# A planner in place of a hand-written order: recorded calls, byte-level dependences, steps placed by urgency

## Chip, cores and metric

One core of a Trainium2 chip runs the kernel. The metric is the device time of one launch in microseconds (us); the time of a kernel is the median of its runs. A core has five engines that work side by side, each through its own queue in order: TensorE (PE) for matrix products, VectorE (DVE), ScalarE (ACT), GpSimd (POOL), and SyncE (SP), which here issues nearly all transfers (DMA). An engine waits on semaphores for what others produce, and everything behind a waiting instruction on the same engine waits with it. Matrix products are written to PSUM, eight banks of 128 partitions by 512 floats; everything else on chip lies in SBUF.

## What is computed

A gated feed-forward layer with quantization, for 4 batches of 1024 tokens, D = 512, FF = 2048:

```python
scale = cond @ norm_w.T + 1.0
ms = jnp.mean(x * x, axis=-1, keepdims=True)
h = x * (scale[:, None, :] * jax.lax.rsqrt(ms + EPS))
u = h @ up_w.T                                  # 512 -> 2 * 2048
val, gate = jnp.split(u, 2, axis=-1)
h = val * jax.nn.gelu(gate, approximate=False)
hq = act_quant(h)                               # per token: 127 / max|h|, rounded
wq = weight_quant(down_w)                       # -1, 0, 1 times mean|down_w|
y = hq @ wq.T                                   # 2048 -> 512
return y + x
```

## The kernel before

Values for the first product are split in two f16 parts (high and low), so that one product takes several f16 matmuls. The weights `up_w` are scaled by powers of two, transposed and split while the first batch runs, and kept in DRAM (`s_dram`) for the later batches, from where they are loaded block by block into `SXY`.

The first batch multiplies directly (`plain`, L577; `plain_first`, L620). Its 16 column blocks j are walked by `first_batch(j)`, which also prepares the weights of blocks to come, the quantized `down_w` (L439, L440), and the tokens of the second batch (`Tokens`: `norm`, `scale`, `high`, `low`, `turn`). The later three batches use a Strassen scheme with seven products of 6 matmuls for each block (`slot(g)`, products at L562); PSUM banks have the tags A (2 buffers), B (1), E (2) and po (3). Each slot takes about 9 us of PE and has three places x, y and z at which other work is woven in: the largest magnitude per token (`pair_max`, L691 to L698), quantizing the batch before (`quant_scale` L754, `quant_round` L758, `quant_up` L762, `quant_down` L766), the token steps of the next batch, and in slots 10 to 13 the down products of the batch before (`Pair`, L833).

The order is written out by hand. The functions are called in the order in which every engine is to carry out its steps, and `Filler` queues distribute DVE's and ACT's lesser steps over slots by budgets in microseconds (`SLOT_US = 9.07`, for example). SP's transfers stand in the same order.

Some steps that the text below speaks of:

- At the start (L879 to L992): x is loaded, its squares are summed (`first_sum`, L899), a small Newton step gives the row factors (`rsqrt_start`, the last line is L911), `first_scale` (L916 and L918) scales four blocks of tokens, one of them on POOL, `first_turn` (L923) transposes them on PE into the banks `ptx`, `w_scale` (L295 on ACT, L297 on POOL) scales the first weights. `keep_warm` (L939) lets PE multiply zeros meanwhile.
- `plain_half`: the products of a half block, then `ACT` with Gelu (L601), then DVE's product of value and gate (L605), which reads PSUM. In the slots the same is done at L640 to L679 (L660 reads the bank A of the block before).
- `token_max` (L712): the largest magnitude over partitions, an all-reduce on POOL, two for a batch (halves h = 0 and 1). `token_scale` (L717, L723) turns it into quantizing factors on DVE.
- `get_ready` (L705): an all-reduce of a 1-element tile `ready`, whose result nothing reads. It is called in slot 0 of the second batch and in the last slot of each of the later batches.
- `Tokens.norm` sums squares on ACT (L496) and takes the root on POOL (L466, L467); `Tokens.scale` goes on with ACT (L504) and POOL (L506) or DVE (L509). `Tokens.low` is L545.

Tiles come from pools with rings of buffers for each tag; semaphores are set by the framework from the accesses of each tile.

Of the kernel before, what the change touches and what calls it, by code (L numbers as in the profile page):

```python
# [1 line left out]

# [44 lines left out]
}  # L47


@with_exitstack  # L50
def glu_quant_kernel(
    ctx: ExitStack,
# [6 lines left out]
    out: bass.AP,  # L59
):  # L60
    nc = tc.nc
    PE, ACT, DVE, POOL, SP = nc.tensor, nc.scalar, nc.vector, nc.gpsimd, nc.sync
    B, S, D = x.shape
    C = cond.shape[1]
    FF = down_w.shape[1]
# [7 lines left out]
    xv = xf.rearrange("(b h a r) d -> b a r h d", b=B, h=2, a=NA)  # L73

    cpool = ctx.enter_context(tc.tile_pool(name="const", bufs=1))
    sm = ctx.enter_context(tc.tile_pool(name="small", bufs=2))
    wpool = ctx.enter_context(tc.tile_pool(name="work", bufs=2))
    psum = ctx.enter_context(tc.tile_pool(name="psum", bufs=2, space=PSUM))

    ident = cpool.tile([P, P], F32, name="ident")  # L80
    neghalf = cpool.tile([P, 4], F32, name="neghalf")
# [70 lines left out]
    def po_bank(name, shape=None):  # L152
        return bank("po", 3, shape, name)
# [553 lines left out]
    def am_tile(b):  # L707
        return wpool.tile([P, 2 * TOK], F32, name=f"am_{b}", tag="am", bufs=1)
# [59 lines left out]
    def rows_of(b, h, a):  # L768
        r = b * S + h * TOK + a * P
        return slice(r, r + P)  # L770
# [18 lines left out]
    def down_end(b, h, a, po, xr, dq, c=slice(None), eng=SP):  # L789
        n = h * NA + a  # L790
        DVE.scalar_tensor_tensor(xr, po, dq[:, n : n + 1], xr, ALU.mult, ALU.add)
        eng.dma_start(out=of[rows_of(b, h, a), c], in_=xr)
# [86 lines left out]
    DVE.memset(eps, EPS)  # L879
# [79 lines left out]
    am = w_largest(0, 1, 2)  # L959
# [317 lines left out]
    for b in range(1, B):  # L1277
        dve, act = Filler(), Filler()
        gains(b)
        am = am_tile(b - 1)  # L1280
# [14 lines left out]
        steps = {}  # L1295
        pairs = {}
        if b + 1 < B:
# [185 lines left out]
    work = list(half_steps(0))  # L1483
# [27 lines left out]
    work = [f for _, f in token_scale(1, am)] + [lambda: token_turn(b, am, 1, 2)]  # L1511
    work += list(half_steps(1))
    bring_dq = [token_undo(b, dq, 0, 1)]
    for h in range(2):
# [15 lines left out]
        work = []  # L1530
# [12 lines left out]
_INS = ["x", "cond_256", "L0_cond_norm_w", "L0_cond_up_w", "L0_cond_down_w"]  # L1543
_OUTS = [((4, 1024, 512), "float32")]
# [23 lines left out]
```

## Time and profile before

| | |
|---|---|
| time, median of 3 runs | 737.53 us (736.88 to 738.68) |
| span of the profiled execution | 734.4 us |
| its own time | not given apart from the three runs; their median lies 3.1 us above the span |
| PE busy | 723.1 us (98% of the span), granted clock 1.000 |
| DVE, ACT, POOL busy | 597.2, 391.0, 200.3 us |
| bytes moved | 115.73 MB, mean 158 GB/s |

The span runs from the first to the last instruction. Busy is the time in which an engine carried out at least one instruction. A waiting list names for each pair of places how long the first stood until the second released it: total us, how many times, the longest. In rows of the timeline the first number is the start and the second the duration, both in us; x12 means that many instructions merged into one row, and the bracket gives the idle time of the engine just before and what ended it. A q behind an engine's name (POOLq) means its instruction queue. `<-issue` stands for idle time for which the profile shows no releaser.

### The profile page before, as it was taken

The numbers are of one execution on the slowest core, as the hardware profiler recorded it, in microseconds if no ns is written. First come the engines' busy times: TensorE is split into PE (matmuls) and PEld (weight loads), VectorE is DVE, ScalarE is ACT, GpSimd is POOL, SyncE is SP. The second block draws the span as 40 slices with busy tenths as digits, with TensorE's granted clock in tenths as the row PEclk, the third lists the DMA queues.
The fourth block names the chain that finished last, engine by engine and source line by source line (L and its number), as shares of the span: only waits on it lengthen the run. The fifth ranks groups of instructions, "written<-read, shape, count | busy, mean of one in ns | idle before, by whom it ended". The sixth has DMA issues, their size and how long they took to land.

```text
span 734.4 us, 10192 instructions
## 1 busy us (share of the span) xinstructions
PE 723.1 (98%) x3684; PEld 361.6 (49%) x3684; DVE 597.2 (81%) x833; ACT 391.0 (53%) x635; POOL 200.3 (27%) x213
## 2 busy tenths in 40 slices
PE   7999999999999999999999999999999999999997
PEld 3554444444444445665444445666444444445744
DVE  6968989877888899797689887787678888755897
ACT  5768657664235676535335666453433665332274
POOL 1487947886100031450010030461020000000100
PEclk9999999999999999999999999999999999999999
DMA  7759989998433545777833556757933445542253
GB/s 232 251 201 135 285 240 244 255 252 222 137 101 99 130 104 172 172 173 172 207 101 100 130 101 171 179 148 164 232 108 102 92 99 104 103 103 90 92 182 115
DMA packets 179566, 115.73 MB, mean 158 GB/s; under 512 B 141750, under 2 KB 147767, under 8 KB 179516
## 3 DMA queue, kind: packets, MB, share of 16 engines
q1 hardware_dynamic: 179226, 114.76, 60.8%
q8 instruction: 29, 0.48, 0.3%
q10 hardware_dynamic: 290, 0.33, 0.2%
q14 instruction: 21, 0.17, 0.1%
HBM read 58.93 MB, written 23.09 MB: 112 GB/s over the span
## 4 chain that ended last, share of the span: by engine, by line
PE 90%; DVE 5%; DMA 2%; POOL 1%; ACT 1%; issue 1%; SPq 0%; DVEq 0%; POOLq 0%
PE A L562 34%; PE E L562 17%; PE po L833 8%; PE B L562 8%; PE pv L577 7%; PE pg L577 7%; PE po_end L782 4%; PE po L782 1%; DMA H<-in_x_dram 1%; PE pw L305 1%; DMA sc<-rows_dram 1%; DVE H L320 1%; DVE nx L545 1%; DVE wam L269 1%; DVE H L605 1%
## 5 line engine op out<-in xcount | busy, mean ns | idle before, releaser
L562 PEld LDWEIGHTS <-SXY 128*128 128x128 f16 x2016 | 197.3, 98 | 232.2 <-issue 0.6
L562 PE MATMUL A<-R,SXY 128*128 128x512 f16 x1152 | 266.2, 379 | 0.0
L562 PE MATMUL E<-R,SXY 128*128 128x512 f16 x576 | 140.0, 379 | 0.1
L660 DVE SCALAR_TENSOR_TENSOR H<-A,sg,t 128x512 f32<-128x512 f32 x48 | 36.0, 750 | 73.2 <-PE A L562 73.0
L712 POOL PARTITION_ALL_REDUCE am<-R x8 | 14.4, 1795 | 232.0 <-DVE R L698 232.0
L754 DVE TENSOR_TENSOR H<-H,am 128x1024 f32<-128x1024 f32 x64 | 76.2, 1217 | 0.0
L577 PEld LDWEIGHTS <-SXY 128*128 128x128 f16 x462 | 45.2, 98 | 55.5 <-issue 1.7
L673 ACT ACTIVATE t<-t,sg 128x512 f32<-128x512 f32 x48 | 34.6, 721 | 69.0 <-DVE t L670 68.8
L562 PE MATMUL B<-R,SXY 128*128 128x512 f16 x288 | 70.0, 379 | 0.0
L696 DVE TENSOR_REDUCE gm<-H 128x512 f32<-128x1024 f32 x56 | 69.0, 1231 | 1.0
L577 PE MATMUL pg<-R,SXY 128*128 128x512 f16 x252 | 57.8, 379 | 0.0
L833 PE MATMUL po<-wd,R 128*128 128x256 fp8e4 (+1 forms) x448 | 56.8, 275 | 0.0
L833 PEld LDWEIGHTS <-R 128*128 128x128 bf16 (+1 forms) x480 | 47.0, 98 | 12.8
L657 ACT ACTIVATE t<-B,sg 128x512 f32<-128x512 f32 x48 | 33.0, 688 | 35.9 <-PE B L562 35.9
L466 POOL TENSOR_SCALAR ssq<-ssq 128x2 f32<-128x2 f32 x12 | 3.2, 268 | 176.5 <-ACT xt L496 124.1
L577 PE MATMUL pv<-R,SXY 128*128 128x512 f16 x210 | 49.9, 379 | 1.1 <-DVE H L605 1.1
L640 ACT COPY t<-A 128x512 f32<-128x512 f32 x48 | 28.0, 583 | 39.8 <-PE A L562 39.4
L648 ACT COPY B<-A 128x512 f32<-128x512 f32 x48 | 27.4, 572 | 38.4 <-PE A L562 38.0
L762 ACT ACTIVATE H<-H 128x1024 f32<-128x1024 f32 x38 | 39.9, 1050 | 14.2 <-DVE H L754 14.1
L652 ACT COPY v<-E 128x512 f32<-128x512 f32 x48 | 28.1, 586 | 31.6 <-PE E L562 27.8
L577 PEld LDWEIGHTS <-R 128*128 128x128 f16 x282 | 27.6, 98 | 34.7 <-issue 2.6
L698 DVE TENSOR_TENSOR R<-R,gm 128x512 f32<-128x512 f32 x56 | 42.3, 755 | 1.3
(203 smaller groups left out, 1013.4 us busy)
## 6 DMA issues: line engine op xcount, KB each, us to landing
SXY<-s_dram SPq DMA_DIRECT2D x66, 256.0 KB, 3.4
SXY<-s_dram SPq DMA_DIRECT2D x18, 384.0 KB, 3.2
H<-in_L_cond_up_w_dram SPq DMA_DIRECT2D x13, 512.0 KB, 3.8
s_dram<-SXY SPq DMA_DIRECT2D x14, 384.0 KB, 3.1
xr<-in_x_dram SPq DMA_DIRECT2D x19, 256.0 KB, 3.0
out_dram<-xr SPq DMA_DIRECT2D x19, 256.0 KB, 2.4
H<-in_x_dram SPq DMA_DIRECT2D x8, 512.0 KB, 5.6
R<-in_L_cond_down_w_dram SPq DMA_DIRECT2D x8, 512.0 KB, 6.7
```

What stands on the lines that cost most here:

```text
L562: PE.matmul(o, s[:, w, k, :], tv[:, :, c, l, k, :], start=start and n == 0, stop=stop and n == len(TERMS) - 1, skip_group_check=True,)
L577: PE.matmul(ps, a[k // 2][:, w, k % 2, :], XP[:, l, k, h * TOK : (h + 1) * TOK], start=n == 0, stop=n == len(terms) - 1,)
L652: ACT.copy(cur["v"], cur["E"])
L657: ACT.activation(cur["t1"], pb, AF.Gelu, scale=gain(g, 1))
L660: DVE.scalar_tensor_tensor(h_half(g - 1, 0), prev["A"], gain(g - 1, 0), prev["t1"], ALU.mult, ALU.mult)
L673: ACT.activation(prev["t2"], prev["t2"], AF.Gelu, scale=gain(g - 1, 1))
L696: DVE.tensor_reduce(gm[0], v, AX.X, ALU.max, apply_absolute_value=True)
L698: return [largest, lambda: DVE.tensor_tensor(m, m, gm[0], ALU.max)]
L754: DVE.tensor_tensor(v, v, r.to_broadcast([P, 2, TOK]), ALU.mult)
L762: ACT.activation(v, v, AF.Copy, bias=MAGIC)
L782: PE.matmul(po.rearrange("p (y c o) -> p y c o", c=2, o=P), q[:, a, h, j], wd8[:, :, j // n, j % n, :, y0:y1].rearrange("p c o y -> p y c o"),
L833: PE.matmul(po, w[:, j], m, start=start and j == 0, stop=stop and j == n - 1, skip_group_check=True,)
```

## The change

The engines are replaced by recorders. Every call (`PE.matmul(...)`, `SP.dma_start(...)`) is written down as a step with its line, its operands, a price in microseconds, and the earlier steps that it depends on, by which 64-byte pieces of a tile (1024-byte pieces of DRAM) they write and read. At the end of the kernel `order` plans all steps six times over and keeps the plan whose PE ends first, and `emit` issues the steps in the order of planned start. The calls themselves and their recorded order stay as they were. The pools become `Rings`, which hand out the same numbers of buffers as fixed tiles.

In a round, `needed` gives each step its latest time: for PE the start in the round before, for other steps the end of the plan, and for all of them no later than what their users need. `place` takes the steps by that time. PE's steps are put one behind another; a step of another engine goes to the first gap on its engine that holds it, from the end of its last operand on. A transfer takes a gap on SP for its issue, and one on a single line of transfers.

```diff
-    PE, ACT, DVE, POOL, SP = nc.tensor, nc.scalar, nc.vector, nc.gpsimd, nc.sync
+    book = Plan()
+    PE, ACT, DVE, POOL, SP = book.engines(nc)
...
-    sm = ctx.enter_context(tc.tile_pool(name="small", bufs=2))
-    wpool = ctx.enter_context(tc.tile_pool(name="work", bufs=2))
-    psum = ctx.enter_context(tc.tile_pool(name="psum", bufs=2, space=PSUM))
+    banks = ctx.enter_context(tc.tile_pool(name="psum", bufs=1, space=PSUM))
+    sm = Rings(cpool, {})
+    wpool = Rings(cpool, {"xn": 1024, "xt": 1024, "am": 1024, "nx": 1792, "v": 512, "gm": 512})
+    psum = Rings(banks, {"A": 512, "B": 512, "E": 512, "po": 512})
...
-    ctx.enter_context(tc.manual_schedule())
     start_t = sm.tile([P, 1], F32, name="start_t", bufs=1)
...
     down_end(b, h, a, po, xr[:, c], dq, c, ACT)
+    ctx.enter_context(tc.manual_schedule())
+    book.emit(book.order())
...
+class Plan:
...
+    def add(self, eng, method, real, args, kwargs):
...
+        s.cost, s.wait = price(eng, method, writes, reads, args, kwargs)
...
+        f = args[2] if method == "activation" else None
+        if f in (AF.Sqrt, AF.Gelu):
+            if f != self.table[0]:
+                deps.update(self.table[1])
+                self.table = f, []
+            elif self.table[1]:
+                deps.add(self.table[1][0])
+            self.table[1].append(s.n)
...
+    def needed(self, clock):
+        for s in reversed(self.steps):
+            s.late = clock if s.eng != "PE" else s.start
+            for t in s.after:
+                s.late = min(s.late, t.late - lag(s, t) - s.wait - s.cost)
+
+    def place(self):
+        steps = self.steps
+        used = {e: Line() for e in ("PE", "ACT", "DVE", "POOL", "SP", "DMA")}
+        last = 0.0
+        for s in sorted(steps, key=lambda s: (s.late, s.n)):
+            t = max((steps[d].end + lag(steps[d], s) for d in s.deps), default=0.0)
+            if s.eng == "PE":
+                t = max(t, last)
+                last = t + s.cost
+                s.start, s.end = t, last
+                continue
+            s.start = used[s.eng].put(t, s.cost)
+            s.end = s.start + s.cost
+            if s.wait:
+                s.end = used["DMA"].put(s.start + 1.2, s.wait) + s.wait + LANDING
+        return last
...
+ROUNDS, LANDING = 6, 1.5
...
+def price(eng, method, writes, reads, args, kwargs):
...
+    if eng == "PE":
+        f32 = any(v.dtype == F32 for v in reads)
+        return (max(n, 64) * (2 if f32 else 1) / 2.4 + 2.5) / 1e3, 0.0
+    if eng == "ACT":
+        return 0.1 + wide * 0.00092 + (0.07 if method != "copy" else 0) + (0.2 if "accum_out" in kwargs else 0), 0.0
+    if eng == "DVE":
+        if wide <= 32:
+            return 0.2, 0.0
...
+        if method == "tensor_tensor" and not psum:
+            if all(v.dtype in (BF16, F16) for v in reads):
+                return 0.1 + wide * 0.0006, 0.0
+            if out.dtype == F16:
+                return 0.1 + wide * 0.0013, 0.0
+        return 0.1 + wide * 0.00107, 0.0
+    if eng == "POOL":
+        if method == "partition_all_reduce":
+            return 1.8 if wide > 1 else 0.4, 0.0
...
```

Here `n` and `wide` are elements for each partition, of the result and of the widest operand. `lag` is 0.2 us after PE, 0.08 us ahead of POOL, 0.05 us elsewhere, and 0 within an engine.

More of the change, by code (lines that the diff above doesn't have):

```diff
@@ L1 @@
+import bisect
+import sys
+import types
 from contextlib import ExitStack
@@ L47, with _runs @@
 }
+GRAIN = 64
+def _runs(v):
+    name, dims, size = v.name, list(v.ap), mybir.dt.size(v.dtype)
+    if str(v.space).endswith("DRAM"):
+        base = v.offset
+        free = dims
+        grain = 1024
+    else:
+        base = v.offset % dims[0][0] if dims[0][0] else v.offset
+        free = dims[1:]
+        grain = GRAIN
+    free = sorted((abs(s), n) for s, n in free if n > 1 and s)
+    run = size
+    while free and free[0][0] * size <= run:
+        s, n = free.pop(0)
+        run = max(run, s * size * (n - 1) + run)
+    starts = [base * size]
+    for s, n in free:
+        starts = [a + s * size * i for a in starts for i in range(n)]
+    return name, {g for a in starts for g in range(a // grain, (a + run - 1) // grain + 1)}
@@ new lines, in _free, with _at_line, call, __init__ @@
+def _free(v):
+    n = 1
+    for d in v.shape[1:]:
+        n *= d
+    return n
+def _at_line(line):
+    def call(method, args, kwargs):
+        return method(*args, **kwargs)
+    return types.FunctionType(call.__code__.replace(co_firstlineno=line - 1), globals())
+class Step:
+    __slots__ = (
+        "n", "eng", "do", "args", "kwargs", "line", "cost", "wait", "deps", "after", "late", "start", "end",
+    )
+class Engine:
+    def __init__(self, plan, name, real):
+        self._plan, self._name, self._real = plan, name, real
+    def __getattr__(self, method):
+        real = getattr(self._real, method)
+        def record(*args, **kwargs):
+            self._plan.add(self._name, method, real, args, kwargs)
+        return record
@@ new lines, with __init__, put, lag @@
+ROUNDS, LANDING = 6, 1.5
+class Line:
+    def __init__(self):
+        self.spans = []
+    def put(self, t, cost):
+        v = self.spans
+        n = bisect.bisect_right(v, (t, 1e9))
+        if n and v[n - 1][1] > t:
+            t = v[n - 1][1]
+        while n < len(v) and v[n][0] < t + cost:
+            t = v[n][1]
+            n += 1
+        v.insert(n, (t, t + cost))
+        return t
+def lag(s, t):
+    if s.eng == t.eng:
+        return 0.0
+    if s.eng == "PE":
+        return 0.2
+    return 0.08 if t.eng == "POOL" else 0.05
```

112 lines of the change are left out of this document (added).

## The prediction

> **What bounds the kernel now.** I read the page's first lines, then who TensorE (PE) waited for, then the busy time by stretches of 20 us, and last the timeline of the places at which PE stood.
>
> ```profile
> span 734.4 us, 10192 instructions
> PE 723.1 (98%) x3684; PEld 361.6 (49%) x3684; DVE 597.2 (81%) x833; ACT 391.0 (53%) x635; POOL 200.3 (27%) x213
> ...
> PE pv L577 <- DVE H L605: 3.2, 4, 1.8
> PE ptx L923 <- DVE wam L147: 1.8, 1, 1.8
> PE pz L939 <- DVE eps L879: 1.4, 1, 1.4
> PE pg L620 <- ACT SXY L329: 0.7, 1, 0.7
> PE pg L620 <- ACT R L927: 0.2, 1, 0.2
> ...
> core 0: us, PE busy (x) PEld busy (x) DVE busy (x) ACT busy (x) POOL busy (x), PEclk, DMA share, GB/s
> 0.00:20.00 20.00, 15.76 (x74) 7.77 (x75) 14.07 (x62) 12.45 (x26) 3.18 (x8) 1.00 0.77 241
> 100.00:120.00 20.00, 17.24 (x79) 7.62 (x78) 19.73 (x24) 9.90 (x16) 17.14 (x18) 1.00 0.76 199
> 120.00:140.00 20.00, 19.60 (x92) 8.79 (x90) 17.91 (x22) 15.37 (x25) 15.85 (x16) 1.00 1.09 265
> ```
>
> PE is busy for 723.1 of 734.4 us, and an order can't make its 3684 matmuls fewer. What is left is 11.3 us: 4.2 in the first 20 us, 2.8 and 0.4 in the two stretches around 120 us, and the tail after the last matmul:
>
> ```profile
> 730.59 0.48 DVE L791 SCALAR_TENSOR_TENSOR R<-po_end,dq_end,R 128x256 f32<-128x256 f32 x1 [0.89 <-PE po_end L782]
> 731.11 0.35 ACTq L792 DMA_DIRECT2D out_dram<-R  x1
> ```
>
> The tail of about 3.8 us (734.4 less 730.6) is one DVE step and one transfer, which no order shortens. So the most that placing can win is the 3.2 us that PE waits for DVE at L605 (PSUM is not yet read out because DVE is behind) and something of the start. Against this stands everything that the planner doesn't know of. The median of the runs is 737.53; no separate time is given for the profiled execution, so I take 737.5 for it, 3.1 us over its span, and do the sum on the span.
>
> **What the planner does.** PE's steps keep about the order in which they are recorded, and every other step goes to the first free gap on its engine after its operands are ready, the most urgent first. Within an engine the result is still one fixed queue: a step that is late in truth holds all behind it. Its prices are close to the trace for the large steps (a 512-wide matmul 215.8 ns; 12 of them take 2.59 us in the chain of waits, `PE A L562 x12`). I look for steps whose true cost isn't in a price.
>
> ```profile
> 196.80 2.59 PE A L562 x12
> ```
>
> **The start: POOL's code.** `get_ready` (L705) is a 1-element all-reduce that the hand order puts ahead of the real all-reduces of L712. The trace shows what it is for:
>
> ```profile
> L705 POOLq MODIFY_POOL_CONFIG  x6: 6/13/18, 178.6 to 498.6; - x6
> L466 POOLq MODIFY_POOL_CONFIG  x4: 88/88/88, 202.7 to 373.9; - x4
> 177.76 0.67 POOL L369 TENSOR_TENSOR R<-H,R 128x256 f16<-128x256 f32 x1
> 184.54 0.38 POOL L705 PARTITION_ALL_REDUCE ready<-ready  x1 [6.11 <-issue]
> 198.47 1.81 POOL L712 PARTITION_ALL_REDUCE am<-R  x1 [13.55 <-DVE R L698]
> ...
> 334.74 0.38 POOL L705 PARTITION_ALL_REDUCE ready<-ready  x1 [6.45 <-issue]
> ```
>
> After ordinary steps the first all-reduce comes 6.11 to 6.45 us late, waiting for nothing but the configuration change ahead of it; the change back (L466) follows the last all-reduce. The same can be seen at the very start for ordinary steps:
>
> ```profile
> L918 POOLq MODIFY_POOL_CONFIG  x2: 11/11/11, 0.8 to 0.8; - x2
> L918 POOLq EVENT_SEMAPHORE  x1: 2574/2574/2574, 7.7 to 7.7; - x1
> 10.09 0.16 DVE L911 SCALAR_TENSOR_TENSOR rs<-newton,rs 128x4 f32<-128x4 f32 x1
> 10.43 0.91 POOL L918 TENSOR_SCALAR H<-H,rs 128x512 f32<-128x512 f32 x1 [10.00 <-DVE rs L911]
> 10.82 1.97 PE L923 MATMUL ptx<-ident,H 128*128 128x128 f32 x16 [1.80 <-DVE wam L147]
> 11.32 0.70 POOL L297 TENSOR_SCALAR H<-H,iv 128x512 f32<-128x512 f32 x1
> 13.90 0.39 PE L620 MATMUL pg<-R,SXY 128*128 128x512 f16 x1 [0.68 <-ACT SXY L329]
> ```
>
> The configuration for ordinary steps is asked for at 0.8 and POOL's queue goes on at 7.7: 6.9 us, hidden today because rs comes at 10.25.
>
> Now the change. The four `get_ready` calls depend on `ready` alone, and nothing depends on them. The planner therefore gives them the last urgency, and then the first gap on POOL that holds 0.4 us, which is the start, where POOL has nothing until L918. All four move there, past everything that POOL does. POOL's true queue is then: load for the all-reduce from 0.8, 6.1 to 6.9 us; four all-reduces at 0.38, 1.5 us; load for ordinary steps, 6.1 to 6.9 us; and only then L918, at 14.5 to 16.1 instead of 10.43. That is 4.1 to 5.7 late; I take 5.0. L918 scales one of the four blocks whose transposes (L923) fill each `ptx` bank, and L297 scales the first weights, so the first product at 13.90 waits for both, and PE has nothing else to do. Cover: none. **+5.0**, bounds 0 (the change back is instant, which the trace can't tell, since POOL has nothing to do for long after it) and 5.7.
>
> **The wait for DVE around 100 to 132 us.**
>
> ```profile
> 106.49 1.48 DVE L284 TENSOR_SCALAR sg<-sw,dx 128x2 f32<-128x2 f32 x1
> 112.42 2.67 DVE L545 TENSOR_TENSOR nx<-xt,nx 128x1024 f16<-128x1024 f32 x1
> 115.00 0.74 DVE L605 SCALAR_TENSOR_TENSOR H<-pv,sg,g 128x512 f32<-128x512 f32 x1
> 115.80 2.75 PE L577 MATMUL pv<-R 128*128 128x512 f16 x12 [1.78 <-DVE H L605]
> ```
>
> L605 is what PE waits for, and L545 is wanted only in the next batch. By urgency L605 goes first wherever it is ready, which removes the 1.78 us and its like. But a step isn't interrupted once begun, and the planner prices this L545 at 1.43 and the 2-element L284 at 0.2, where the trace has 2.67 and 1.48 (POOL is busy 17.14 of those 20 us). Part of the wait stays: **-2.5**, bounds -3.2 and 0. A later start of PE helps too, since weights arrive meanwhile.
>
> **The later all-reduces.** With `get_ready` gone from its places, L712 itself asks for the load. It is free if POOL has been idle some 6.5 us before L712 is ready, as in 178 to 198 now. But the planner also pulls ordinary steps ahead: the token steps of the next batch run as soon as their buffers are free, where the hand order has them here:
>
> ```profile
> 258.48 0.19 POOL L466 TENSOR_SCALAR ssq<-ssq 128x2 f32<-128x2 f32 x1 [55.77 <-ACT xt L496]
> ...
> 367.63 1.81 POOL L712 PARTITION_ALL_REDUCE am<-R  x1 [32.51 <-DVE R L698]
> 373.84 0.75 DVE L660 SCALAR_TENSOR_TENSOR H<-A,sg,t 128x512 f32<-128x512 f32 x1 [1.77 <-PE A L562]
> 376.23 2.75 PE L562 MATMUL A<-R,SXY 128*128 128x512 f16 x12
> ```
>
> If these fall close to an all-reduce, before 198 or 367, a load of 6.1 to 6.9 us is exposed, and DVE's L717, next in its queue, holds the PSUM read-outs behind it. The read-out L660 ends at 374.59, and its bank is written again by the second half of the 12 matmuls from 376.23, at 377.5: 2.9 us to spare. An exposed load so costs PE 0 to 3.5 us each, not its whole length. Two boundaries at 1 each: **+2**, bounds 0 and 7. The third I take as covered, its token steps being over long before.
>
> **Remaining differences.** ACT's table load for Gelu, SP's one queue of transfers and DVE's short steps at 0.2 cost something where the plan left no room: **+1**, bounds -1 (transfers earlier) and 4. The sum: 734.4 + 5.0 - 2.5 + 2 + 1 = 739.9, and 3.1 around it give 743.0. With all lower bounds it is 733.3, with all upper ones 754.2.
>
> **One rule of the skill against this change.** The start of the trace has PE slow at first and then fast:
>
> ```profile
> 3.55 2.31 PE L939 MATMUL pz<-H 128*128 128x512 f16 x5
> 7.34 1.69 PE L939 MATMUL pz<-H 128*128 128x512 f16 x7
> ```
>
> The five warm-up matmuls at 3.55 take 0.46 us each, the seven at 7.34 take 0.24. Here PE's longest pause after that is 1.8 us; in the changed kernel it would stand from about 12 to 16 or 17. If that sends it back to 0.46, then at most the 5.9 us that it needed here (1.4 to 7.34) run at half speed: up to +2.9, so 745.9 in place of 743.0. The Trainium skill (TensorE: Matmul & The Clock Gate, "What's actually happening") says that an idle window of about 3.4 us halves the clock until as long a busy one has passed; by that figure I estimate +1.7, and no run here shows it yet.
>
> **Rivals.** First, faster: the loads stay covered, because the change back is instant, and L605 no longer waits. 737.5 - 3.2, and about 0.9 from the two short waits at L620, is 733.4. For it: prices that fit the trace; against it: the 6.9 us at the start.
>
> Second, no difference: 737.5. Either gains and losses cancel, or the planner ends near the hand's order because the recorded order and its buffers leave little freedom.
>
> Third, clearly slower by one mechanism: ACT stands behind POOL at the turn of a batch. A token step's scale (L504) waits for rs of POOL:
>
> ```profile
> ACT xn L504 <- POOL rs L467: 6.7, 2, 3.9
> 204.61 0.59 ACT L640 COPY t<-A 128x512 f32<-128x512 f32 x1 [1.84 <-PE A L562]
> 205.71 2.75 PE L562 MATMUL A<-R,SXY 128*128 128x512 f16 x12
> ```
>
> The copy L640 ends at 205.20 and PE goes on with that bank at 205.71, so ACT has about 0.5 us to spare. If the plan puts token norms right after an all-reduce, rs comes a load later than planned, 6.1 to 6.9 us, L504 stands at ACT's head and the copies behind it stop PE for some 6 us. It decides from about 1 us of lateness on. Once on top of my sum this is 749; at two turns 755.
>
> **How the numbers follow.** A difference of 0.3%, 2.2 us, is about what a measurement of this kernel can tell from none. My case, 740 to 748 around **743.0**: 0.40. ACT behind POOL, or several such places, 748 to 760: 0.22. No difference: 0.13. Faster: 0.25. So faster 0.25, same 0.13, slower 0.62. For eight in ten the range goes from 733.0, into the faster case, to 755.0, the second turn of the third rival; cases of both signs lie in it, and the likeliest alone is 740 to 748.
>
> **What would show it.** Right: four L705 rows within the first 10 us, POOL's L918 at 14 us or later and L620 as late; PE's waits for L605 below 3.2 us; the L712 rows with idle time that ended by issue. Wrong: L918 near 10.4, or L705 rows elsewhere, or PE's idle total beyond 20 us with its waits in the middle of a batch, which would mean that prices or transfers, not POOL's code, decide.

## The result and the profile after

The changed kernel takes **768.72 us** (median of 4 runs, 768.16 to 769.44); the kernel before, run beside it, takes 737.75 (736.88 to 738.68). The ratio is 1.042 (95% interval 1.040 to 1.043): slower, by 31 us. The profiled execution has a span of 767.7 us, 33.3 more than before. The first lines of the page of after:

```profile
span 767.7 us, 10236 instructions
PE 731.1 (95%) x3684; PEld 363.3 (47%) x3684; DVE 610.8 (80%) x833; ACT 392.4 (51%) x635; POOL 209.6 (27%) x213
```

The number of matmuls is the same, but PE is busy for 8.0 us more (731.1 against 723.1); in part because some of them ran at a lower clock. The other 25.3 us are idle time (36.6 against 11.3). Whom PE waited for (total us, times, longest):

```profile
PE E L836 <- DVE t L944: 9.3, 1, 9.3
PE E L851 <- DVE H L879: 5.8, 10, 1.3
PE A L836 <- DVE H L934: 4.7, 1, 4.7
PE A L477 <- DVE mx L470: 4.4, 1, 4.4
PE po L1107 <- ACT po L1133: 2.5, 2, 1.6
```

Two single waits of 9.3 and 4.7 us stand in the slots (L836 is L562 of before). The wait for DVE in the first batch, which the prediction wanted to see shrink, grew from 3.2 us to 5.8 (L851 is L577, L879 is L605).

Where in time the loss lies is read from the starts of PE's rows. *First product* is the start of the first matmul of the first batch's product; *first batch* goes from there to the first of the 2016 matmuls of the slots; a *turn* is the first eight slots of the second, third and fourth batch (336 matmuls each), in which the batch before is quantized; *rest* is all else.

| kernel, times in us | first product | first batch | turn 1 | turn 2 | turn 3 | rest | span |
|---|---|---|---|---|---|---|---|
| before | 13.9 | 177.6 | 72.5 | 72.5 | 72.5 | 325.4 | 734.4 |
| after | 18.8 | 182.8 | 81.2 | 84.8 | 72.5 | 327.6 | 767.7 |
| difference | +4.9 | +5.2 | +8.7 | +12.3 | 0.0 | +2.2 | +33.3 |

**The turns.** POOL's timeline of after, around the first two turns:

```profile
203.77 2.66 POOL L986 PARTITION_ALL_REDUCE am<-R  x1 [10.13 <-DVE R L972]
213.97 0.18 POOL L740 TENSOR_SCALAR ssq<-ssq 128x2 f32<-128x2 f32 x1 [7.53 <-issue]
214.23 0.74 POOL L741 TENSOR_TENSOR rs<-ssq,neghalf 128x2 f32<-128x2 f32 x1
220.72 1.80 POOL L986 PARTITION_ALL_REDUCE am<-R  x1 [5.75 <-issue]
...
391.16 1.80 POOL L986 PARTITION_ALL_REDUCE am<-R  x1 [5.86 <-issue]
399.66 3.98 POOL L780 TENSOR_TENSOR xn<-xn,sc 128x512 f32<-128x512 f32 x2 [6.70 <-ACT B L922]
...
413.78 1.80 POOL L986 PARTITION_ALL_REDUCE am<-R  x1 [5.99 <-issue]
```

In the first turn the planner put the root of a token step (L740, L741: less than 1 us of work) between the two all-reduces of the batch. Each change between an ordinary step and an all-reduce shows the wait for POOL's code that before had only ahead of `get_ready`: 7.53 us to L740, then 5.75 to the second all-reduce. In the second turn there are three (5.86, up to 6.70, and 5.99). DVE's queue has the scaling of the all-reduce's result (L991) ahead of the step that reads out PSUM, and PE waits for that one. DVE, then PE, each with the two turns:

```profile
222.56 0.43 DVE L991 TENSOR_SCALAR am<-am 128x512 f32<-128x512 f32 x1 [5.97 <-POOL am L986]
222.90 0.74 DVE L934 SCALAR_TENSOR_TENSOR H<-A,sg,t 128x512 f32<-128x512 f32 x1
...
415.62 0.43 DVE L991 TENSOR_SCALAR am<-am 128x512 f32<-128x512 f32 x1 [8.40 <-POOL am L986]
415.96 0.68 DVE L944 TENSOR_TENSOR t<-E,t 128x512 f32<-128x512 f32 x1
```

```profile
217.52 1.46 PE L836 MATMUL A<-R,SXY 128*128 128x512 f16 x6
223.70 2.72 PE L836 MATMUL A<-R,SXY 128*128 128x512 f16 x6 [4.72 <-DVE H L934]
226.21 2.31 PE L836 MATMUL E<-R,SXY 128*128 128x512 f16 x6
228.36 1.46 PE L836 MATMUL B<-R,SXY 128*128 128x512 f16 x6
...
416.70 2.72 PE L836 MATMUL E<-R,SXY 128*128 128x512 f16 x6 [9.25 <-DVE t L944]
```

Six matmuls take 1.46 us; after a pause of 4.72 or 9.25 us the next six take 2.72. That is the slower clock. Of the 8.0 us of extra busy time 5.4 lie in these two turns (74.9 and 75.5 us busy, against 72.5 each); nearly all the rest comes before the slots. In the stretches of 20 us the granted clock is the number after the engines, 0.83 and 0.81:

```profile
220.00:240.00 20.00, 16.30 (x66) 6.96 (x66) 16.70 (x20) 5.97 (x10) 8.77 (x7) 0.83 0.26 68
...
400.00:420.00 20.00, 10.75 (x43) 4.44 (x42) 11.34 (x13) 3.39 (x6) 9.52 (x7) 0.81 0.17 47
```

**The start.** The answers for the lines of `get_ready` (L979) and of POOL's first scale (L1191, once L918), with duration in ns and first and last start:

```profile
L979 POOL PARTITION_ALL_REDUCE ready<-ready x4: 350/354/385, 3.6 to 5.0; - x4
L979 POOLq MODIFY_POOL_CONFIG  x2: 11/11/11, 0.8 to 0.8; - x2
...
L1191 POOLq MODIFY_POOL_CONFIG  x2: 83/83/83, 5.2 to 5.3; - x2
L1191 POOLq EVENT_SEMAPHORE  x1: 3022/3022/3022, 9.0 to 9.0; - x1
L1191 POOL TENSOR_SCALAR H<-H,rs x1: 682/682/682, 15.5 to 15.5; 128x512 f32<-128x512 f32 x1
```

All four 1-element all-reduces stand at the start, as predicted, and POOL's first scale runs at 15.5 instead of 10.43.

### The profile page after: what moved, and what is told of

It is laid out like the page before. It is cut to its first block, busy times and chain, and to the rows that moved or that the text cites. A ratio compares the mean times of both kernels' runs of the same rounds, so it can differ in the third digit from the quotient of the medians.

```text
span 767.7 us, 10236 instructions
## 1 busy us (share of the span) xinstructions
PE 731.1 (95%) x3684; PEld 363.3 (47%) x3684; DVE 610.8 (80%) x833; ACT 392.4 (51%) x635; POOL 209.6 (27%) x213
## 4 chain that ended last, share of the span: by engine, by line
PE 61%; DVE 5%; issue 2%; POOL 2%; ACT 0%; POOLq 0%; DVEq 0%; ACTq 0%
PE A L836 28%; PE E L836 14%; PE B L836 7%; PE po L1107 7%; PE po L1056 2%; PE E L1056 1%; PE A L1056 1%; DVE gm L970 1%; DVE nx L819 1%; POOL xn L780 1%; DVE H L1083 1%; POOL am L986 0%; DVE R L972 0%; PE B L1107 0%; PE B L1056 0%
## 5 line engine op out<-in xcount | busy, mean ns | idle before, releaser
L836 PEld LDWEIGHTS <-SXY 128*128 128x128 f16 x2016 | 198.4, 98 | 251.6 <-issue 22.9
L836 PE MATMUL A<-R,SXY 128*128 128x512 f16 x1152 | 268.0, 381 | 6.2 <-DVE H L934 4.7
L836 PE MATMUL E<-R,SXY 128*128 128x512 f16 x576 | 142.1, 383 | 9.3 <-DVE t L944 9.3
L1028 DVE TENSOR_TENSOR H<-H,am 128x1024 f32<-128x1024 f32 x64 | 77.8, 1245 | 0.1
L851 PEld LDWEIGHTS <-SXY 128*128 128x128 f16 x462 | 45.2, 98 | 59.6 <-issue 6.6
L947 ACT ACTIVATE t<-t,sg 128x512 f32<-128x512 f32 x48 | 34.6, 722 | 73.7 <-DVE t L944 73.7
L836 PE MATMUL B<-R,SXY 128*128 128x512 f16 x288 | 71.3, 384 | 0.0
L740 POOL TENSOR_SCALAR ssq<-ssq 128x2 f32<-128x2 f32 x12 | 2.8, 234 | 218.1 <-ACT H L770 132.0
L851 PE MATMUL E<-R,SXY 128*128 128x512 f16 x210 | 49.9, 379 | 4.1 <-DVE H L879 4.1
L950 DVE TENSOR_TENSOR v<-A,v 128x512 f32<-128x512 f32 x48 | 33.1, 690 | 24.5 <-PE A L836 22.9
L944 DVE TENSOR_TENSOR t<-E,t 128x512 f32<-128x512 f32 x48 | 33.0, 688 | 21.7 <-PE E L836 21.4
L926 ACT COPY v<-E 128x512 f32<-128x512 f32 x48 | 28.1, 586 | 31.4 <-PE E L836 25.3
L851 PEld LDWEIGHTS <-R 128*128 128x128 f16 x282 | 27.5, 98 | 35.1 <-issue 3.3
```

Source lines behind the costliest of these rows:

```text
L836: PE.matmul(o, s[:, w, k, :], tv[:, :, c, l, k, :], start=start and n == 0, stop=stop and n == len(TERMS) - 1, skip_group_check=True,)
L851: PE.matmul(ps, a[k // 2][:, w, k % 2, :], XP[:, l, k, h * TOK : (h + 1) * TOK], start=n == 0, stop=n == len(terms) - 1,)
L944: DVE.tensor_tensor(prev["t2"], prev["E"], prev["t2"], ALU.add)
L947: ACT.activation(prev["t2"], prev["t2"], AF.Gelu, scale=gain(g - 1, 1))
L950: DVE.tensor_tensor(cur["v"], cur["A"], cur["v"], ALU.add)
L1028: DVE.tensor_tensor(v, v, r.to_broadcast([P, 2, TOK]), ALU.mult)
```

## Experiments

All times are medians; a ratio is against runs of the kernel before on the same chip. The table shows the stages of all of them; the turns are the three of the table above.

| kernel | time | ratio, 95% | first product | first batch | turns 1 / 2 / 3 |
|---|---|---|---|---|---|
| e10_same_order_no_loads | 749.87 | 1.017 (1.0155 to 1.0185) | 19.3 | 182.4 | 74.2 / 72.5 / 72.5 |
| e5_before_between | 753.89 | 1.021 (1.018 to 1.024) | 14.3 | 178.6 | 77.2 / 76.8 / 79.1 |
| e1_code_groups | 768.67 | 1.042 (1.040 to 1.043) | 19.2 | 182.9 | 86.0 / 79.3 / 72.5 |
| e2_groups_priced | 754.44 | 1.022 (1.020 to 1.024) | 20.7 | 181.5 | 77.3 / 74.2 / 72.5 |
| e3_no_ready | 769.28 | 1.044 (1.041 to 1.046) | 17.8 | 182.6 | 82.0 / 83.5 / 72.5 |
| e4_before_ready_first | 742.78 | 1.008 (1.006 to 1.010) | 18.6 | 177.0 | 72.5 / 72.5 / 72.5 |
| e7_start_loads_recorded | 763.51 | 1.036 (1.034 to 1.038) | 24.8 | 186.8 | 76.2 / 72.5 / 72.5 |
| e9_start_by_hand | 769.75 | 1.042 (1.039 to 1.045) | 19.3 | 182.7 | 81.4 / 85.0 / 72.5 |
| e6_prices_up | 750.59 | 1.018 (1.0155 to 1.020) | 18.6 | 175.3 | 73.2 / 73.4 / 72.6 |
| e8_combined | 748.63 | 1.0155 (1.014 to 1.017) | 25.4 | 174.4 | 73.7 / 73.0 / 72.5 |
| e12_first_prices | 766.96 | 1.039 (1.035 to 1.042) | 18.4 | 192.3 | 72.5 / 83.1 / 72.5 |
| e13_scatter_held | 768.87 | 1.042 (1.040 to 1.044) | 18.0 | 182.9 | 82.1 / 83.4 / 72.5 |
| e11_repaired | 741.76 | 1.0053 (1.004 to 1.007) | 17.2 | 180.9 | 72.8 / 72.5 / 72.5 |
| e14_repaired_again | 741.72 | 1.005 (1.0035 to 1.0066) | 15.1 | 182.0 | 73.7 / 72.5 / 72.5 |
| e15_no_higher_prices | 750.04 | 1.016 (1.014 to 1.018) | 14.9 | 191.6 | 72.5 / 72.9 / 72.5 |

### The turns: is it POOL's code?

**e10_same_order_no_loads** keeps the changed kernel's plan on every engine and puts ordinary steps in the place of the all-reduces, so that POOL's code never changes. What it leaves out is the maximum over partitions. The steps put in are about as long as an all-reduce (1.04 to 1.95 us at the turns, where an all-reduce takes 1.8 to 2.7).

```diff
-        POOL.partition_all_reduce(am[:, c], m_view(b, h), P, bass_isa.ReduceOp.max)
+        POOL.tensor_tensor(am[:, c], m_view(b, h), m_view(b, h), ALU.add)
```

> The order of the planner's kernel on every engine, step for step, but POOL's all-reduces are replaced by ordinary additions of a tile to itself (the 1-element ones by multiplications), at the same prices to the planner. No code has to be changed on POOL. What is left out is the maximum over partitions: the quantizing factors are then each partition's own. Theory (code loads): the two turns lose no more than 1 us each, of 8.7 and 12.3, and the start gains 1 as without the 1-element all-reduces: 745 to 749. What stays is the start (about 4) and the first batch (5.2). Rivals (prices, queue heads, transfers): 760 or more, as the order is the same.

The time falls from 768.72 to 749.87, and the turns from 81.2 and 84.8 to 74.2 and 72.5. In the list of PE's waits the two long ones are gone, and those of the first batch and the start stay:

```profile
PE E L851 <- DVE H L879: 5.6, 10, 1.3
PE A L477 <- DVE mx L470: 4.8, 1, 4.8
```

So the changes of POOL's code are the cause at the turns: 19.3 of 33.3 us in the spans, about 19 of 31 in the medians. The 1.7 us that turn 1 still loses (74.2 against 72.5) are not POOL's code.

**e5_before_between** takes the other direction: the hand order with one 2-element step on POOL between the two all-reduces. The condition in the edit holds for all three turns, not for the two that the expectation names.

```diff
         POOL.partition_all_reduce(am[:, c], m_view(b, h), P, bass_isa.ReduceOp.max)
+        if h == 0 and b < B - 1:
+            POOL.tensor_scalar(spare, spare, 1.0, 1.0, ALU.mult, ALU.mult)
```

> The kernel before, with one POOL step on 2 elements (0.2 us) put between the two all-reduces of each of the first two turns and nothing else changed. Theory A (what costs at the turns is an ordinary step between the two all-reduces, since it makes two code loads of 6 to 8 us each one behind the other and PE then idles long enough to be clocked down): each of the two turns gets 6 to 12 us longer, 750 to 762. Theory B (the lateness of the second all-reduce is mostly covered by what DVE and PE can still do): 0 to 3 us each, 738 to 744.

A step of 0.19 us costs 16 us in three turns, 4.6, 4.3 and 6.6 in the spans. POOL's timeline shows the first of them:

```profile
199.88 1.81 POOL L714 PARTITION_ALL_REDUCE am<-R  x1 [13.22 <-DVE R L698]
208.97 0.19 POOL L716 TENSOR_SCALAR spare<-spare 128x2 f32<-128x2 f32 x1 [7.27 <-issue]
215.77 1.80 POOL L714 PARTITION_ALL_REDUCE am<-R  x1 [6.62 <-issue]
```

Before, the second all-reduce followed the first after 2.46 us (198.47 and 200.93); here after 15.89. The time is inside the first theory's range, but that range was meant for two turns, and the first two cost less than its 6 to 12 each: PE's waits there stay at 2.0 us or less, and the six matmuls behind the longest still take 1.46, so there the clock holds. In the third turn a wait of 2.62 us follows, and six take 2.51:

```profile
219.64 1.46 PE L562 MATMUL A<-R,SXY 128*128 128x512 f16 x6 [2.00 <-DVE H L660]
...
573.81 2.51 PE L562 MATMUL E<-R,SXY 128*128 128x512 f16 x6 [2.62 <-DVE t L670]
```

**e1_code_groups** and **e2_groups_priced** make the planner keep POOL's steps in groups of one code, in recorded order; e2 adds a price for each change.

```diff
+        if eng == "POOL":
+            code = method == "partition_all_reduce"
+            if code != self.code[0]:
+                deps.update(self.code[1])
+                self.code = code, []
+                s.cost += 6.5          # e2 alone
+            elif self.code[1]:
+                deps.add(self.code[1][0])
+            self.code[1].append(s.n)
```

> The planner's kernel with one more kind of dependence: POOL's all-reduces and its ordinary steps keep the recorded order of the changes between them, as Sqrt and Gelu do on ACT already. No price is added. Theory (POOL's code loads): the two waits of 4.7 and 9.3 us, the slow clock behind them and the 3.5 us by which POOL is late at the start go, about 27 of the 31 us lost: 741 to 745; up to 752 if the load back to ordinary steps, still without a price, holds ACT at a token step. Rival (prices of DVE and ACT too low, queue heads late everywhere): the losses at the turns of the batches stay, 757 or more. Rival (transfers late): 765 or more.

> As the run with code groups, and the first step after each change is priced 6.5 us higher. Theory (code loads): 739 to 743, at most 1 us slower than without the price and up to 8 faster where the load back was exposed. Rival (prices of DVE and ACT): no different from the run without the price, and both 757 or more. Rival (transfers): 765 or more.

Groups alone win nothing (768.67): the wait moves from DVE to ACT. PE's waits in e1:

```profile
PE A L845 <- ACT t L923: 10.2, 1, 10.2
...
PE B L845 <- ACT B L931: 4.9, 1, 4.9
```

The token norms now come right after the second all-reduce, their rs comes a code load later than planned, and ACT stands with the copies of PSUM behind it. With the price in the plan, ACT's place is planned for it: 754.44, turns 77.3 and 74.2. What is left of the turns there is again ACT (4.4 us in two waits).

### The start: POOL's code, the plan, or both?

**e3_no_ready** takes the four all-reduces out of the changed kernel (`get_ready` does nothing); **e4_before_ready_first** puts them first in the hand order.

> The planner's kernel without the four 1-element all-reduces. Nothing else on POOL is changed. Theory (code loads): POOL's first ordinary step starts as soon as the row factors are there, 12.1 us instead of 15.5, and the first product some 2.5 to 3.5 us earlier; the turns of the batches are as before: 765 to 766. If the start is set by the transfers of x and not by POOL: 768 to 769, no change.

> The kernel before, in the hand's order, with only the four 1-element all-reduces moved to the start. As the prediction has it, two loads of POOL's code one after the other hold L918 back by 4.1 to 5.7 us: 741.5 to 743.5. If the first load is short, as the planner's kernel suggests (all-reduces at 3.6 us), by 2 to 4: 739.5 to 742. If loads at the start are covered: no change, 737 to 739. The later all-reduces ask for their load themselves, POOL having been idle for long, and cost nothing in each case.

```diff
+    for _ in range(4):
+        get_ready()
...
-            if j == NJ - 1:
-                get_ready()
-            elif b == 1 and j == 0:
-                get_ready()
```

e4 costs 5.6 us (742.78 against 737.16), and the first product comes at 18.6 instead of 13.9, waiting for POOL: the predicted mechanism is real and has about the predicted size. POOL's first scale is 4.0 us late there (14.40 against 10.43). The slower clock accounts for the rest: eight transposes ahead of PE's pause take 1.09 us, the eight behind it 1.97:

```profile
10.91 1.09 PE L925 MATMUL ptx<-ident,H 128*128 128x128 f32 x8 [1.55 <-DVE wam L147]
15.14 1.97 PE L925 MATMUL ptx<-ident,H 128*128 128x128 f32 x8 [3.14 <-POOL H L920]
```

But e3, without the four all-reduces, wins only 1.0 us of the start (17.8), and nothing in time. So the plan delays the start by a second cause which the first one covers.

**e7_start_loads_recorded** (groups and prices of e2, with the first ten transfers of SP in recorded order) tried to find it among SP's transfers, and missed:

```diff
+        first = [s for s in self.steps if s.eng == "SP"][:10]
+        for n, s in enumerate(first):
+            s.late = -100.0 + n
```

> The kernel with code groups and prices (754.4), where the first ten transfers of SP are issued in the recorded order, norm_w first, then x, then the first weights. If the start is set by where norm_w lands (10.6 us there, 3.8 in the hand's order), the first product comes at 14 to 15.5 instead of 20.7 and the time is 748 to 750. If the start is set by something else, 753 to 755.

The small transfer of cond on ACT's queue fell behind these ten on the planner's one line of transfers, and the first product came at 24.8. This says nothing of the cause.

**e9_start_by_hand** keeps all steps recorded before the first product in their order; `get_ready` still goes to the start:

```diff
+        if self.start and "dma" not in method:
+            if eng in self.last:
+                deps.add(self.last[eng])
+            self.last[eng] = s.n
...
+        for s in self.steps[: self.begun + 1]:
+            s.late = s.n - 1e4
```

> The changed kernel, with the steps recorded before the first product kept in their recorded order on every engine and every queue of transfers; the four get_ready still go to the start of POOL. Theory A (the start's 4.9 us have two causes that hide each other, POOL's code and the planner's order of the start): POOL's code alone now holds the start, so the first product comes at about 18.6 us, as in the hand order with get_ready first, and nothing is won: 766 to 770. Theory B (the planner's order of the start is what costs): the first product comes at 14 to 15 us and the time is 763 to 765.

First product at 19.3: with POOL's code there, the order of the rest of the start changes nothing. **e11_repaired** has the same start with POOL's groups, so that `get_ready` stays in its places (the other edits of it are told below): 17.2. And **e14_repaired_again** holds one more transfer, the broadcast of cond. In the hand order it stood in ACT's queue at 13.28, behind the first read-outs of PSUM; the planner sends it at 1.35, as nothing in the operands forbids that.

```diff
+        if self.start and eng == "ACT" and "dma" in method and "ACT" in self.last:
+            deps.add(self.last["ACT"])
```

ACT's queue, first e11, then e14:

```profile
1.35 0.36 ACTq L467 DMA_DIRECT2D R<-in_cond_dram  x1
```

```profile
14.51 0.35 ACTq L474 DMA_DIRECT2D R<-in_cond_dram  x1
```

The first product comes at 15.1. So with the start in recorded order, taking POOL's code out of it gives 2.1 us (e9 to e11, which differ in more, but not in the start), and moving the broadcast 2.0 more (e11 to e14); 1.2 over the 13.9 of before stay without a cause that was tried. As e3 and e9 show, taking away either cause alone wins little.

### The first batch: prices or transfers?

In the first batch DVE has little room: of the 10 us from 110 to 120 it is busy for 9.90, before and after. **e6_prices_up** raises the planner's prices of DVE, ACT and POOL by 10% everywhere, **e12_first_prices** in the first batch alone; **e8_combined** is e7 with the price for the change back at 9.0 and the 10% in the first batch.

```diff
+        if self.first and eng in ("DVE", "ACT", "POOL"):
+            s.cost *= 1.1
```

> The planner's kernel with every price of DVE, ACT and POOL raised by 10%. Theory (code loads): the four 1-element all-reduces still go to the start and token steps still fall between the two all-reduces of a batch, so waits ended by issue remain at L989 or so and the time is 758 to 775. Rival (prices too low): with room in the plan the waits of PE shrink to a few us, 745 or less.

> As the run with the recorded start, with the change of POOL's code priced at 6.5 us to the all-reduce and 9 us back, and the prices of DVE, ACT and POOL 10% higher in the first batch alone. First product at 14 to 15.5, first batch 175 to 177 us (181.5 without the higher prices, 175.3 with them in all batches), turns no more than 2 us over the hand's: 737 to 742, so about the hand's time or up to 4 us over.

> The changed kernel, with the planner's prices of DVE, ACT and POOL 10% higher for the steps of the first batch alone, nothing else. Theory A (the first batch is lost to prices that are too low while all engines work): the stretch from the first product to the second batch's first matmul takes 174 to 177 us instead of 182.8, the start is unchanged (18.8), and the turns lose what the loads happen to expose, 0 to 25 us in all, as their place is not under control: 740 to 765. Theory B (it is lost to the start's transfers and not to prices): the stretch stays at 181 to 184.

e6: 182.8 falls to 175.3, 2.3 us better than the hand; e8 against e7: 186.8 to 174.4. PE's waits for DVE's read-out (L879 of after) are gone from both lists. That e6 is 18 us faster in all is not the prices' doing alone: in this plan no token step fell between two all-reduces, and its last stage lost 6.5 us (PE from the last slot on: 49.9 us against 43.4), as PE now waits for rounding on ACT and DVE. e12 missed: 192.3. One wait made it, of 10.86 us at 62 us, before the transposes of a block of weights. The transfers issued in 40 to 66 us of e12 (KB each, median us to landing), and then the weights in the same stretch of after:

```profile
H<-in_L_cond_up_w_dram SPq DMA_DIRECT2D x2, 512.0 KB, 20.1
...
rows_dram<-scT SPq DMA_DIRECT2D x3, 2.0 KB
```

```profile
H<-in_L_cond_up_w_dram SPq DMA_DIRECT2D x3, 512.0 KB, 12.7
```

Three transfers of single elements (2 KB each) went out at 44.8 to 46.4 beside the weights, which took 20.1 us; in after 12.7, where the median of such blocks over the whole span is 4.6. In the hand order they go at 59.4. That gave a new theory: the planner prices such a transfer at 1.4 us, and the weights are late behind them in the changed kernel too. **e13_scatter_held** lets them go only when the product recorded before them is done; on the chip one went out at 55.9 us and two at 63.6:

```diff
+        if eng == "PE":
+            self.pe = s.n
+        if self.hold:
+            deps.add(self.pe)
...
+        book.hold = True
         for b in range(1, B):
             SP.dma_start(out=rows_dram[b].rearrange("(k p) -> p k", p=P), in_=scT[:, :, b])
+        book.hold = False
```

> The changed kernel, with one dependence more: the three transfers of single elements (rows_dram<-scT), which the planner sends at 44 us, wait for the product that is recorded before them, and so go out at about 60 us, as in the hand order. Theory A (the first batch is lost because the weights stand behind these transfers, DVE is idle for 8 us from 52.9 and then late for the rest of the batch): that idle stretch is gone and the stretch from the first product to the second batch takes 176 to 179 us instead of 182.8. Theory B (it is lost to prices of DVE and POOL that are too low): 181 to 184. In both the start keeps its 18.8 and the turns lose what the loads happen to expose.

The stretch 50 to 60 us by engines (PE, PEld, DVE, ACT, POOL busy), after and then e13, which has 80 to 90 us as well:

```profile
50.00:60.00 10.00, 10.00 (x52) 4.99 (x51) 2.49 (x7) 1.51 (x3) 7.49 (x10) 1.00 0.73 136
```

```profile
50.00:60.00 10.00, 10.00 (x52) 5.08 (x51) 9.34 (x22) 7.82 (x16) 6.77 (x9) 1.00 0.46 164
80.00:90.00 10.00, 9.81 (x47) 4.32 (x46) 2.43 (x5) 3.51 (x6) 2.46 (x4) 1.00 0.85 281
```

DVE's hole is filled, 2.49 to 9.34 us, as the theory says, and the first batch still takes 182.9: PE waits 6.3 us for DVE where it waited 5.8. But another hole opened: DVE is busy for 2.43 us of 80 to 90 (8.77 in after), behind ACT, which stands for a transfer (`SXY<-H`). So e13 moved the idle time and does not decide. What speaks against the theory is e8: DVE has a hole there too, 1.97 us busy of 60 to 70, and its first batch is the shortest of all, 174.4.

**e11_repaired**, **e14_repaired_again** and **e15_no_higher_prices** put everything together: the start of e9, POOL's groups with prices of 6.5 and 9.0, higher prices for 16-bit additions and 1-element activations, and the 10% in the first batch, which e15 leaves out again; e14 and e15 have the two held transfers.

> The planner with everything repaired that the runs so far name: the start in recorded order; POOL's steps in groups between changes of code (so get_ready stays in its place before the all-reduces), the first step after a change priced 6.5 us more (to an all-reduce) or 9.0 us more (back); prices of DVE, ACT and POOL in the first batch 10% higher; 16-bit additions of DVE and the 1-element activations of ACT priced as the traces have them. Theory A (unpriced code loads, the start and too low prices in the first batch make up the loss): first product at 13.9 to 14.5 us, first batch 174 to 176 (hand 177.6), turns at most 2 over the hand's 72.5 each, the rest 0 to 2 over: 734 to 739, so the hand's time or a little better. Theory B (a plan made ahead loses against the chip's variation wherever it packs steps tightly, whatever the prices): it stays at 744 to 750, with the loss spread over short waits of PE.

> The repaired planner (start in recorded order, groups and prices for POOL's code, 10% on the prices in the first batch) with two dependences more: the broadcast of cond (R<-in_cond_dram) keeps its place on ACT's queue behind the first read-outs, and the transfers of single elements wait for the product recorded before them. Theory A (what the first repaired planner lacked was the place of these two transfers): first product at 13.9 to 14.6 us instead of 17.2, first batch 174 to 178 instead of 180.9, turns as there: 732 to 738. Theory B (the start is held by the order of PE's own steps, and the first batch by DVE): 16.5 to 17.5 and 179 to 182, so 740 to 743.

> As e14_repaired_again, but without the 10% on the prices in the first batch. Theory A (the first batch is lost to the weights that stand behind the transfers of single elements, not to prices): within 2 us of e14_repaired_again, first batch 174 to 178. Theory B (the prices of DVE and POOL are too low there): first batch 180 to 184 and PE waits for DVE in it, 5 us in all or more, as in the changed kernel: 740 to 746.

PE's longest waits in e14, then in e15:

```profile
PE E L885 <- DVE H L913: 4.2, 2, 3.4
```

```profile
PE E L883 <- DVE H L911: 10.5, 7, 3.9
```

The prices are worth 9.6 us of the first batch here (191.6 against 182.0). The longest wait of both kernels is something else, though. In e14, DVE and then PE:

```profile
85.86 0.50 DVE L548 TENSOR_SCALAR sc<-sc,ux 128x512 f32<-128x512 f32 x1 [7.69 <-DMA sc<-rows_dram]
...
87.07 5.28 PE L885 MATMUL E<-R 128*128 128x512 f16 x12 [3.45 <-DVE H L913]
```

DVE stood 7.69 us for the load of cond's scale, which reads what the held transfers write, and the read-out L913 stood behind it in DVE's queue. Twelve matmuls then take 5.28 us, against 2.75 before the pause. That one place accounts for about 6 us, more than the 4.4 by which e14 lies behind the hand in this stage; e15 has the same wait, 3.88. e11, which does not hold the transfers, has no such wait, but one of 3.3 us before transposes of weights.

In all four pairs PE's waits for DVE's read-out in the first batch fall with the higher prices: 5.8 us to none (e6), 4.7 to none (e8 against e7), 5.8 to 2.5 (e12), and 10.5 to 4.2 (e14 against e15; without the two waits for the load, 6.6 to 0.8). The stage gains 7.5, 12.4 and 9.6 us in three of them and loses 9.5 in e12, by its one late block of weights; in e7 a wait of 4.0 us before transposes of weights is part of the 12.4. The record of after also shows two kinds of DVE steps whose price is off (from 20 to 201 us; the number behind the busy time is the mean in ns):

```profile
L713 DVE TENSOR_SCALAR R<-R,wsc 128x1024 f32<-128x1024 f32 x8 | 11.1, 1391 | 0.0
L819 DVE TENSOR_TENSOR nx<-xt,nx 128x1024 f16<-128x1024 f32 x4 | 9.7, 2420 | 0.0
```

The planner has them at 0.80 and 1.43 us. So prices that are too low, DVE's above all, are the best supported cause of these waits; late transfers are a second loss, which several plans bring in anew. That a flat 10% is the remedy is not shown, nor what the prices of ACT and POOL do in it: no run raised one engine's prices alone. With turns and rest at the hand's level, the repaired planner comes to 741.7, 0.5% behind the hand order; no version here beats the kernel before.

## Why the prediction was wrong

The sign was right, the size was not: 743.0 foretold, 768.72 measured, beyond the upper end of 755. By its own terms, in spans: 734.4 + 5.0 - 2.5 + 2 + 1 against 734.4 + 4.9 + 5.2 + 21.0 + 2.2.

- **Start, +5.0, measured +4.9.** All that it named came: the four all-reduces first, POOL's first scale in the window of 14.5 to 16.1 (15.49). The size is right partly by luck. The first load, put at 6.1 to 6.9 us, cost nothing that shows: in e4 the configuration stands at 0.8 and the first all-reduce at 1.5. The way back took 10.3 us instead from the configuration to the first scale (5.2 to 15.49), and 11.3 in e4 (3.1 to 14.4); in it POOL's queue stood for rs until 12.0, and in e4 until 10.4. And "Cover: none" was wrong the other way: the planner's own order of the start would have made PE wait almost as long.
- **The wait for DVE, -2.5: the sign failed.** PE's wait for this line grew by 2.6 us (3.2 to 5.8), and the first batch as a whole by 5.2; the rest is busy time (2.0) and lesser waits. The step was "By urgency L605 goes first wherever it is ready, which removes the 1.78 us and its like". The two prices quoted there as too low (L545, L284) were the warning; the prediction took them for a rest of the old wait, where they make new ones: ten in place of four. That prices make them is supported by the lengths and the four pairs above, not shown for each wait.
- **The later all-reduces, +2 with 0 to 7, measured +21.0: the term that decided.** That token steps come close to an all-reduce and expose a load was said. The step that failed is the cost of such a load, "0 to 3.5 us each", taken once for a turn. Three things were missed. The steps fell *between* the two all-reduces of a turn, so that two loads follow each other (e5: 15.89 us between the two instead of 2.46). The room of 2.9 us is that of the PSUM read-out alone; in the hand's order DVE also asks late for the second all-reduce's result, here at 210.33, when it has been there since 202.71:

```profile
210.33 0.36 DVE L717 TENSOR_SCALAR am<-am 128x512 f32<-128x512 f32 x1
```

The plan has L991 straight ahead of the read-out and gives these 7.6 us away. With the hand's order a second all-reduce that comes 13.4 us later costs a turn 4.3 to 6.6 us (e5); in the plan 14.5 and 20.2 us cost 8.7 and 12.3. And the halved clock, weighed for the start alone, came here too: PE is busy 5.4 us longer in the two turns. The third turn was said to be free, and is (72.5).
- **The clock.** The trace of after has six matmuls in 2.72 us behind pauses of 4.72 and 9.25 us; the first whole row at full speed starts 4.7 us after the first of them (223.70 to 228.36). Behind pauses of 2.0 us six still take 1.46 (e5), but behind one of 2.49 twelve take 4.29 (e12):

```profile
201.41 4.29 PE L854 MATMUL E<-R,SXY 128*128 128x512 f16 x12 [2.49 <-DVE H L882]
```

By the Trainium skill (TensorE: Matmul & The Clock Gate, "What's actually happening") an idle window of about 3.4 us halves the clock until a busy one as long has passed. The halving agrees, and the 1.5 us that e12's twelve matmuls lose against 2.75 are what half the clock costs in some 3 us; but a pause of 2.49 us is enough here. At the start the slower clock cost after's first product nothing (five of its matmuls take 1.24 us, as before); in e4, whose start is the one foretold, the transposes lost 0.9.
- **The rest, +1, measured +2.2**, inside its bounds of -1 to 4.
- **The rivals.** ACT behind POOL does not occur in the changed kernel, but is what e1 turns the loss into: 10.2 and 4.9 us, at the place that the prediction named. "Loads stay covered" fell with e10. PE's idle total, 36.6 us, is beyond the 20 that the prediction took for a sign of prices or transfers; e10 shows that POOL's code decided all the same.

## To carry to other kernels

A planner can place steps only by the costs that it is told: before an order written by hand is given up, list what its odd places protect (a dummy all-reduce, a transfer behind a read-out on a queue) and put each into the model as a dependence or a price. A cost of *changing* between kinds of steps belongs to pairs of neighbours and not to a step; kept in groups alone it moved to the next engine (e1's turns lose 20.3 us, after's 21.0), priced as well it mostly went (e2's lose 6.5). Slack that is read from the old order is no bound for a new one: the hand asked for a result 7.6 us late, and the planner had no reason to keep that.

## What the runs showed of the hardware

A change of POOL's code is not one number: to the all-reduce it took 5.75 to 6.9 us in the middle of the kernel, back to ordinary steps 7.3 to 8.1 (7.53 in after, 7.27, 8.09 and 7.48 in e5) and once no more than 6.70, and at the start the first scale ran 3.5 to 4.0 us after its operand was there. An all-reduce as POOL's first step behind its memsets shows no load: in e4 it ran at 1.5, with its configuration at 0.8. The Trainium skill (GPSIMD Engine Reference, "2.1 Instruction dispatch") gives about 6 us for the first call after a load; the way to the all-reduce agrees in the middle of the kernel, the way back is mostly longer.

Three transfers of 2 KB in single elements went with a landing time of 20.1 us for 512 KB of weights in e12, against a median of 4.6 in after over the whole span (12.7 beside the same three transfers); that they cause it was not shown apart.
